# A two-layer graph network: finishing a block of attention by a narrow product, and the loads of the start over other queues

## The chip, the cores and the metric

The kernel runs on one core of a Trainium2 chip. A core has five engines that run their own instruction streams side by side: TensorE (PE: matmuls, and the loads of their stationary operand, PEld), VectorE (DVE), ScalarE (ACT), GpSimd (POOL) and SyncE (SP), which issues most of the DMAs. They share an on-chip memory (SBUF) and a smaller one into which TensorE writes (PSUM[...]). The metric is the device time of one execution in microseconds (us); smaller is better.

## The reference, cut

```python
# x: 3327 x 128, adj: 3327 x 3327 of zeros and ones; all float32
h = maximum(layernorm(x), 0)
deg = adj.sum(axis=1);  deg = where(deg == 0, 1, deg)
g = (adj.T @ h / deg) @ W_n.T + b_n + h @ W_c.T + b_c
x = x + relu(gamma * (g - mean(g)) * rsqrt(var(g) + 1e-5) + beta)   # over the nodes

h = maximum(layernorm(x), 0)
q, k, v = ((h @ W.T).reshape(128, 3327, 8) for W in (Wq, Wk, Wv))
a = einsum('dnh,dmh->dnm', q, k) * 128 ** -0.5 + adj + adj
out = einsum('dnm,dmh->dnh', softmax(a, axis=2), v)
x = x + out.reshape(3327, 1024) @ Wo.T
```

The second layer is an attention with 128 batches of 3327 queries by 3327 keys and only 8 numbers per query and key. Over a billion exponentials are taken, and nearly all of the time lies there.

## The kernel before

**The first layer** loads x, normalises it in 26 chunks of 128 nodes (stats, roots, factors, normalise, lines 342 to 367) and then runs over the 26 row chunks of adj (line 426): each is loaded by SP into one of three buffers, multiplied by TensorE into seven banks, summed by ScalarE and searched for its maximum by VectorE. `beside` adds small work of other kinds to each chunk. The loop over line 380 asks for the statistics of chunk group i + 1 before it normalises group i. All loads of x and of the weights are issued by ScalarE (lines 320 to 334), ahead of its first activation. Then come the batch norm, the residual, the second layer norm and the first projections (lines 461 to 612); `keep_nodes` stores x to the tensor xd, `keep_columns` the normalised x to hd, and the last loop sorts the keys of the first batches into `k`.

**The attention** (line 667) handles four batches at a time: 32 groups i, each of 7 blocks y of 476 queries (the last has 472), each block of 13 steps s. A step handles two chunks of keys, as four pairs of a key chunk and a half (two batches). For each pair TensorE makes the scores in two products of 32 rows (`product`, line 742), in one of three score buffers. Two or three of the four pairs are "plain": VectorE adds a chunk of adj (`add`, line 852), and one ScalarE row, `late`, takes the exponentials of all of them at line 895, one step later. The other one or two are "weighted": ScalarE takes the exponential straight from PSUM (line 861) and GpSimd multiplies by a stored exp(2 adj) (line 864, tile wt, loaded from the tensor wd). Steps 3, 7 and 11 (DOUBLE) have two weighted pairs, the others one. Three steps later (LAG) TensorE multiplies the exponentials by the values into one of two banks av (`weigh`, line 618), with a ninth value column of ones that gives the sum.

The order of the instructions is written out by hand; every engine works its own stream in that order. Within one step it is: the first weighted product and its exponential, `late` of the step before, product and add 0, the first half of the weighting (`second(0)`), product and add 1, the last product, then one `step()` of a finished block if s is in PARTS, the second half of the weighting, and a `begin` or `go_on` of a side job.

A finished block goes through the generator `finish` (line 623), one part per step of PARTS: copy av to SBUF (`avs`, step 3), four transposes that bring every fourth query onto the partitions (line 633, step 5), reciprocal and product with it (lines 640 to 643, result oq, step 7), store (step 8). Transposed, each of 119 partitions holds 128 columns per quarter, of which 4 x 9 mean something.

Side jobs are started in steps 7 and 11 of a block and use the bank av of the block that is being finished: six projections (queries, keys and values) for group i + 2 in blocks 0 to 2, two transposing parts of `outputs` for the group before in block 3, and its last part, the product with Wo in 16 matmul rows (line 277), in step 7 of block 4. In group 0 `more_weights` (line 755) also prepares the wd of the next block: it loads adj into a tile t in one step, takes its exponential on ScalarE in the next (line 770) and stores it in the one after.

SP works its queue in order too: `fetch` loads adj and wt two steps ahead and waits there for a free buffer, and each store waits for what it stores.

Of the kernel before, what the change touches and what calls it, by code (L numbers as in the profile page):

```python
# [9 lines left out]
F32 = mybir.dt.float32  # L10
# [9 lines left out]
D = 128  # L20
H = 8
# [12 lines left out]
CH = 4 * NP // D  # L34
NG = D // G
DOUBLE = (3, 7, 11)
PARTS = (3, 5, 7, 8)

# [8 lines left out]
def tile_two_layer_gnn(  # L47
# [206 lines left out]
    def outputs(wk, j):  # L254

        r = min(CH, N - j * CH)
        t = wk.tile([P, H, D], F32, name="t4")
        nc.sync.dma_start(
            t[:CH].rearrange("p e j -> p (e j)"), atr[j * CH : (j + 1) * CH, :]
        )  # L260
        xj = wk.tile([P, D], F32, name="xj")
        nc.sync.dma_start(xj[:CH], xd[j * CH : (j + 1) * CH, :])
        tT = wk.tile([P, H, P], F32, name="t4")

        def turn(e):
            bank = yield
            pt = bank.rearrange("p (i q) -> p i q", i=4)
            for i in range(4):
                nc.tensor.transpose(pt[:, i, :CH], t[:CH, 4 * e + i, :], ident[:CH, :CH])
            yield  # L270
            nc.vector.tensor_copy(tT[:, 4 * e : 4 * e + 4, :CH], pt[:, :, :CH])
            yield

        def last():
            bank = yield
            for e in range(H):
                nc.tensor.matmul(  # L277
                    bank[:CH, :D], tT[:, e, :CH], wo[:, e, :], start=(e == 0), stop=(e == H - 1)
                )
            yield  # L280
            y = wk.tile([P, D], F32, name="y")
            nc.vector.tensor_add(y[:CH], bank[:CH, :D], xj[:CH])
            yield
            for p0, p1 in pieces(r):
                nc.sync.dma_start(out[j * CH + p0 : j * CH + p1, :], y[p0:p1])

        return [turn(0), turn(1), last()]

    def drive(part, bank=None):

# [7 lines left out]
    with tc.tile_pool(name="l0", bufs=1) as l0, tc.tile_pool(  # L298
# [20 lines left out]

        xr = x[: (NC - 1) * P, :].rearrange("(c p) d -> p c d", p=P)  # L320
        nc.vector.memset(xs[:, NC - 1, :], 0.0)
        for c0, c1 in ((0, 8), (8, NC - 1)):
            nc.scalar.dma_start(xs[:, c0:c1, :], xr[:, c0:c1, :])
        for p0, p1 in pieces(N - (NC - 1) * P):
            nc.scalar.dma_start(
                xs[p0:p1, NC - 1, :], x[(NC - 1) * P + p0 : (NC - 1) * P + p1, :]
            )
        nc.scalar.dma_start(wc, WcT)
        for i, b in enumerate((b_n, b_c, gamma, beta)):
            nc.scalar.dma_start(cols[:, i : i + 1], b.rearrange("o d -> d o"))  # L330
        nc.scalar.dma_start(wn, WnT)
        for t, w in zip(wqk, (WqT, WkT, WvT)):
            nc.scalar.dma_start(t, w)
        nc.scalar.dma_start(wo, WoT.rearrange("(e p) o -> p e o", p=P))

        st = l0.tile([P, NC, 6], F32, name="ln_st")
        mv = l0.tile([P, NC, 2], F32, name="ln_mv")
# [45 lines left out]
        nc.vector.tensor_add(bias, cols[:, 0:1], cols[:, 1:2])  # L383

        def beside(x):

            if x < NQ:
                pt, cs = turned(x, A, aside)
                nc.scalar.copy(B[:, cs, :], pt)
            elif x < 2 * NQ:  # L390
                n0 = (x - NQ) * NB
                w = min(NB, NP - n0)
                nc.tensor.matmul(
                    aside[:, :w], wc, B2[:, n0 : n0 + w], start=True, stop=True
                )
                nc.scalar.activation(
                    C2[:, n0 : n0 + w], aside[:, :w], AF.Identity, bias=bias
                )
            elif x < 2 * NQ + 4:
                i = x - 2 * NQ  # L400
                sq = sp.tile([P, NB], F32, name="sq")
                w = wqk[i // 2][:, i % 2 * NB : (i % 2 + 1) * NB]
                nc.gpsimd.tensor_tensor(sq, w, w, ALU.mult)
                nc.tensor.matmul(aside[:1, :], ones[:, :1], sq, start=True, stop=True)
                nc.vector.tensor_reduce(norm[:, i : i + 1], aside[:1, :], AX.X, ALU.max)
# [128 lines left out]
        def residual(i):  # L534
            pt, cs = turned(i, A, acc[i])
            nc.vector.tensor_add(xs[:, cs, :], xs[:, cs, :], pt)
            if i < 2:
                keep_nodes(cs)

        def second_norm(i, engine):  # L540
# [82 lines left out]
    def finish(rp, av, d0, n0, w):  # L623
# [4 lines left out]
        nc.vector.tensor_copy(avs[:, : R * J], av[:, : R * J])  # L628
        yield

        pt = av.rearrange("p (j q) -> p j q", j=J)
        for j in range(J):
            nc.tensor.transpose(  # L633
                pt[:R, j, :], avs[:, j : j + (R - 1) * J + 1 : J], ident
            )
# [31 lines left out]
    def attention():  # L667


        with tc.tile_pool(name="adj", bufs=4) as ap, tc.tile_pool(  # L670
# [13 lines left out]
            if True:  # L684
# [69 lines left out]

                def more_weights(i, y, s):

                    k, phase = s // 3, s % 3
                    if i or y + 1 >= len(qblocks) or k > 3:
                        return
                    n0, w = qblocks[y + 1]  # L760
                    c = WC + 2 * k
                    n = min(2, NC - c)
                    if phase == 0:
                        have["w"] = wk.tile([P, 2, QB], F32, name="t4")
                        nc.sync.dma_start(
                            have["w"][:, :n, :w], adjr[:, c : c + n, n0 : n0 + w]
                        )
                    elif phase == 1:
                        a = have["w"][:, :n, :w]
                        nc.scalar.activation(a, a, AF.Exp, bias=low, scale=2.0)  # L770
                    else:
                        nc.sync.dma_start(
                            wd[c - WC : c - WC + n, :, n0 : n0 + w].rearrange("c p n -> p c n"),
                            have["w"][:, :n, :w],
                        )

# [53 lines left out]
                for x, (i, y, s) in enumerate(steps):  # L830
# [152 lines left out]
    def general():  # L983
# [65 lines left out]
        with tc.tile_pool(name="gw2", bufs=2) as wk, tc.tile_pool(  # L1049
            name="gp2", bufs=1, space=PSUM  # L1050
        ) as gp:
            banks = [gp.tile([P, NB], F32, name=f"h{i}") for i in range(3)]
# [52 lines left out]
```

## Time and profile before

| | us |
|---|---|
| median of 3 runs | 10390.24 |
| their range | 10385.12 to 10391.82 |
| the profiled execution | 10385.98 |
| its span, first to last instruction | 10384.2 |

| engine | busy us | share of the span |
|---|---|---|
| ScalarE | 9925.5 | 96% |
| TensorE | 9816.7 | 95% |
| VectorE | 9331.0 | 90% |
| GpSimd | 8443.5 | 81% |

A row of the list of groups gives a source line, engine, operation and tiles (written <- read), the shape, how many (x), then busy us and mean ns of one, then the idle time of the engine just before these instructions and what ended it. A row of the list of waits reads: who waited, for whom, us in total, how often, the longest. A row of the timeline reads: start and duration in us, engine, line, operation, tiles, shapes, how many rows are merged in it, and in brackets the engine's idle time before and what ended it. TensorE's durations are modelled and overlap; the distance between starts says more. The TensorE clock was granted at 0.991 of full speed on average.

### The profile page before, as it was taken

The numbers are of one execution on the slowest core, as the hardware profiler recorded it, in microseconds if no ns is written. First come the engines' busy times: TensorE is split into PE (matmuls) and PEld (weight loads), VectorE is DVE, ScalarE is ACT, GpSimd is POOL, SyncE is SP. The second block draws the span as 40 slices with busy tenths as digits, with TensorE's granted clock in tenths as the row PEclk, the third lists the DMA queues.
The fourth block names the chain that finished last, engine by engine and source line by source line (L and its number), as shares of the span: only waits on it lengthen the run. The fifth ranks groups of instructions, "written<-read, shape, count | busy, mean of one in ns | idle before, by whom it ended". The sixth has DMA issues, their size and how long they took to land.

```text
span 10384.2 us, 188013 instructions
## 1 busy us (share of the span) xinstructions
PE 9816.7 (95%) x72431; PEld 2888.6 (28%) x72431; DVE 9331.0 (90%) x9501; ACT 9925.5 (96%) x6655; POOL 8443.5 (81%) x4316
## 2 busy tenths in 40 slices
PE   7899999999999999999999999999999999999998
PEld 3222222222222222222222222222222222222222
DVE  5689999999999999999999999999999999999998
ACT  4789999999999999999999999999999999999998
POOL 1678888888888888888888888888888888888887
PEclk9899999999999999999999999999999999999999
DMA  6765666665666665666655666655666555666554
GB/s 232 205 178 161 164 168 167 168 165 158 168 167 168 167 162 161 168 169 168 167 159 163 168 169 167 164 165 159 171 168 167 162 164 164 169 168 165 159 153 129
DMA packets 1115994, 1735.87 MB, mean 167 GB/s; under 512 B 194606, under 2 KB 1091756, under 8 KB 1107404
## 3 DMA queue, kind: packets, MB, share of 16 engines
q1 hardware_dynamic: 1110558, 1717.86, 60.2%
q8 instruction: 568, 9.31, 0.4%
q10 hardware_dynamic: 4350, 4.20, 0.1%
q14 instruction: 342, 2.80, 0.1%
q0 software_dynamic: 176, 1.71, 0.0%
HBM read 1621.05 MB, written 102.38 MB: 166 GB/s over the span
## 4 chain that ended last, share of the span: by engine, by line
POOL 21%; PE 16%; ACT 8%; issue 5%; DVE 3%; DMA 0%; POOLq 0%; ACTq 0%; SPq 0%; DVEq 0%
POOL f L864 20%; PE av L618 8%; PE s L742 6%; ACT f L861 5%; ACT d L895 3%; DVE d L852 2%; PE av L633 1%; POOL k L192 1%; PE av L208 1%; PE av L277 0%; POOL o L238 0%; POOL o L237 0%; DVE oq L643 0%; DVE ri L641 0%; DVE avs L628 0%
## 5 line engine op out<-in xcount | busy, mean ns | idle before, releaser
L864 POOL TENSOR_TENSOR f<-f,wt 128x952 f32<-128x952 f32 (+1 forms) x3584 | 7944.8, 2235 | 1680.6 <-ACT f L861 1660.7
L852 DVE SCALAR_TENSOR_TENSOR d<-at,s 128x952 f32<-128x952 f32 x8064 | 8754.4, 1140 | 606.2 <-PE s L742 447.7
L895 ACT ACTIVATE d<-d 128x2856 f32<-128x2856 f32 (+1 forms) x2912 | 7055.5, 2423 | 12.5 <-DVE d L852 2.3
L618 PE MATMUL av<-d,v 128*9 128x476 f32 x32256 | 5072.3, 567 | 1.9 <-ACT d L895 1.9
L742 PE MATMUL s<-q,k 32*128 32x476 f32 x23296 | 4108.3, 476 | 407.9 <-ACT f L861 334.1
L861 ACT ACTIVATE f<-s 128x952 f32<-128x952 f32 (+1 forms) x3584 | 3436.4, 980 | 224.7 <-PE s L742 220.9
L742 PEld LDWEIGHTS s<-q,k 32*128 32x128 f32 x23296 | 1772.8, 182 | 5631.8 <-DVE d L852 3296.9
L618 PE MATMUL av<-f,v 128*9 128x476 f32 x14336 | 2853.4, 566 | 0.0
L618 PEld LDWEIGHTS av<-d,v 128*9 128x9 f32 x32256 | 583.6, 88 | 1162.3 <-issue 1131.8
L618 PEld LDWEIGHTS av<-f,v 128*9 128x9 f32 x14336 | 316.6, 88 | 153.1 <-issue 139.6
L192 POOL CAST k<-ks 128x256 fp32r<-128x256 f32 x434 | 284.6, 656 | 0.0
L633 PE MATMUL av<-ident,avs 128*119 128x128 f32 (+1 forms) x896 | 241.3, 392 | 0.8 <-DVE avs L628 0.8
L633 PEld LDWEIGHTS av<-ident,avs 128*119 128x119 f32 (+1 forms) x896 | 198.2, 292 | 52.7 <-issue 51.1
L430 PE MATMUL acc<-a,A 128*128 128x512 f32 (+1 forms) x364 | 151.8, 570 | 23.2 <-ACT A L364 23.1
L238 POOL TENSOR_TENSOR o<-pf,o 104x512 fp32r<-104x512 f32 x124 | 159.9, 1289 | 9.9
L628 DVE COPY avs<-av 128x476 f32<-128x476 f32 (+1 forms) x224 | 144.6, 645 | 4.5 <-PE av L618 4.5
L437 DVE TENSOR_REDUCE amax<-a 128x1 f32<-128x3327 f32 x26 | 93.7, 3611 | 35.3 <-DMA a<-in_adj 35.3
L236 DVE TENSOR_SCALAR pf<-av,low_half 104x512 f32<-104x512 f32 x62 | 46.6, 751 | 72.0 <-PE av L208 70.3
L234 DVE COPY pf<-av 104x512 f32<-104x512 f32 x62 | 42.9, 692 | 73.0 <-PE av L208 71.8
L214 DVE COPY ov<-av 104x512 f32<-104x512 f32 x62 | 42.9, 692 | 67.8 <-PE av L208 67.8
L430 PEld LDWEIGHTS acc<-a,A 128*128 128x128 f32 x364 | 69.0, 192 | 108.3 <-issue 84.7
L770 ACT ACTIVATE t<-t,low_half 128x952 f32<-128x952 f32 (+1 forms) x24 | 26.2, 1090 | 65.4 <-DMA t<-in_adjT 65.4
(121 smaller groups left out, 1022.6 us busy)
## 6 DMA issues: line engine op xcount, KB each, us to landing
at<-in_adjT SPq DMA_DIRECT2D x1728, 476.0 KB
wt<-wd SPq DMA_DIRECT2D x1536, 238.0 KB
at<-in_adjT SPq DMA_DIRECT2D x288, 472.0 KB
wt<-wd SPq DMA_DIRECT2D x256, 236.0 KB
ks<-kT SPq DMA_DIRECT2D x496, 104.0 KB
q<-qT SPq DMA_DIRECT2D x496, 104.0 KB
a<-in_adj SPq DMA_DIRECT2D x26, 1663.5 KB
kT<-o SPq DMA_DIRECT2D x128, 208.0 KB
```

The source lines that it names most:

```text
L192: nc.gpsimd.tensor_copy(k[:, c : c + n, half * 64 : half * 64 + 64], ks.bitcast(F32).rearrange("g (p c) -> g c p", c=NC)[:, c : c + n, :],)
L208: nc.tensor.matmul(bank[:CH], hj, wqk[s][:, e * NB : (e + 1) * NB], start=True, stop=True)
L238: nc.gpsimd.tensor_tensor(o[:CH, 1], f[:CH], o[:CH, 0].bitcast(F32), ALU.subtract)
L430: nc.tensor.matmul(acc[i][:, :w], A[:, c, :], a[:, n0 : n0 + w], start=(c == 0), stop=(c == NC - 1),)
L618: nc.tensor.matmul(av[32 * b : 32 * b + H + 1, :w], tiles[2][:, b, c, :], e, start=first, stop=last,)
L628: nc.vector.tensor_copy(avs[:, : R * J], av[:, : R * J])
L633: nc.tensor.transpose(pt[:R, j, :], avs[:, j : j + (R - 1) * J + 1 : J], ident)
L742: nc.tensor.matmul(p[:, x, :we], k[rs, c, :], q[rs, n0 : n0 + we], start=True, stop=True,)
L852: nc.vector.scalar_tensor_tensor(d[:, j, :, :w], have[0, i, y, c // 2][:, c % 2, :w] .unsqueeze(1).to_broadcast([P, 2, w]), SAFE / 2, p[:, ...
L861: nc.scalar.activation(f[:, :, :w], p[:, :, :w], AF.Exp, scale=2.0)
L864: nc.gpsimd.tensor_tensor(f[:, :, :w], f[:, :, :w], have[1, i, y, c][:, :w].unsqueeze(1).to_broadcast([P, 2, w]), ALU.mult,)
L895: nc.scalar.activation(flat, flat, AF.Exp, scale=2.0)
```

## The change

It has many small parts.

- `finish` replaces the four transposes by four ordinary matmuls against `some`, the 36 of the 128 columns of the identity that are used later, and makes them in two parts of two. PARTS gets a fifth step, 6, for the second.
- In step 7, the second of DOUBLE, `step()` stands before the second product and add instead of behind the last product.
- The last part of `outputs` becomes two, of four matmuls (eight rows) each, with an add of their own.
- `more_weights` takes the exponential in the third step of its three instead of the second, and stores a tile when it loads the next.
- The first four chunks of x are loaded by SP ahead of adj, the rest by ScalarE in other pieces; the weights are loaded by GpSimd; ScalarE's table of roots is loaded by an activation on a constant, ahead of the first that needs it; the sum of the biases moves into `beside`.
- Chunks 8 to 11 of xd are stored with those before them, the rest by GpSimd right after the residual; hd is stored after the sorting of the keys. The loads of the rest of q begin two steps later.

```diff
-PARTS = (3, 5, 7, 8)
+PARTS = (3, 5, 6, 7, 8)
...
-        def last():
+        def last(i):
             bank = yield
-            for e in range(H):
+            for e in range(4 * i, 4 * i + 4):
                 nc.tensor.matmul(
-                    bank[:CH, :D], tT[:, e, :CH], wo[:, e, :], start=(e == 0), stop=(e == H - 1)
+                    bank[:CH, :D], tT[:, e, :CH], wo[:, e, :],
+                    start=(e == 4 * i), stop=(e == 4 * i + 3),
                 )
             yield
-            nc.vector.tensor_add(y[:CH], bank[:CH, :D], xj[:CH])
+            nc.vector.tensor_add(y[:CH], bank[:CH, :D], y[:CH] if i else xj[:CH])
...
-        return [turn(0), turn(1), last()]
+        return [turn(0), turn(1), last(0), last(1)]
...
-        for c0, c1 in ((0, 8), (8, NC - 1)):
+        nc.sync.dma_start(xs[:, :4, :], xr[:, :4, :])
+        for c0, c1 in ((4, 12), (12, NC - 1)):
             nc.scalar.dma_start(xs[:, c0:c1, :], xr[:, c0:c1, :])
...
-        nc.scalar.dma_start(wc, WcT)
+        root = l0.tile([P, 1], F32, name="root")
+        nc.scalar.activation(root, eps, AF.Sqrt)
+        for t, w in zip(wqk, (WqT, WkT, WvT)):
+            nc.gpsimd.dma_start(t, w)
+        nc.gpsimd.dma_start(wc, WcT)
         for i, b in enumerate((b_n, b_c, gamma, beta)):
-            nc.scalar.dma_start(cols[:, i : i + 1], b.rearrange("o d -> d o"))
-        nc.scalar.dma_start(wn, WnT)
-        for t, w in zip(wqk, (WqT, WkT, WvT)):
-            nc.scalar.dma_start(t, w)
-        nc.scalar.dma_start(wo, WoT.rearrange("(e p) o -> p e o", p=P))
+            nc.gpsimd.dma_start(cols[:, i : i + 1], b.rearrange("o d -> d o"))
+        nc.gpsimd.dma_start(wn, WnT)
+        nc.gpsimd.dma_start(wo, WoT.rearrange("(e p) o -> p e o", p=P))
...
-            if i < 2:
+            if i < 3:
                 keep_nodes(cs)
...
+        nc.gpsimd.dma_start(
+            xd.rearrange("(c p) d -> p c d", p=P)[:, 12:, :], xs[:, 12:, :]
+        )
         roots(4, NC)
...
-        keep_nodes(slice(8, NC))
-        keep_columns(0, NQ)
         for x, c in enumerate(range(0, NC, 4)):
...
+        keep_columns(0, NQ)
...
-        pt = av.rearrange("p (j q) -> p j q", j=J)
+        pt = av[:, : J * G * (H + 1)].rearrange("p (j q) -> p j q", j=J)
+
+        some = ident.rearrange("p (b h) -> p b h", h=32)[:, :, : H + 1]
         for j in range(J):
-            nc.tensor.transpose(
-                pt[:R, j, :], avs[:, j : j + (R - 1) * J + 1 : J], ident
-            )
-        yield
-        pv = pt.rearrange("p j (b h) -> p b j h", h=32)
+            nc.tensor.matmul(
+                pt[:R, j, :], avs[:, j : j + (R - 1) * J + 1 : J], some, start=True, stop=True
+            )
+            if j % 2:
+                yield
+        pv = pt.rearrange("p j (b h) -> p b j h", h=H + 1)
...
-                    k, phase = s // 3, s % 3
-                    if i or y + 1 >= len(qblocks) or k > 3:
+                    k, phase = divmod(s, 3)
+                    if i or y + 1 >= len(qblocks):
                         return
                     n0, w = qblocks[y + 1]
                     c = WC + 2 * k
-                    n = min(2, NC - c)
+                    if phase == 0 and k:
+                        nc.sync.dma_start(
+                            wd[c - 2 - WC : c - WC, :, n0 : n0 + w].rearrange("c p n -> p c n"),
+                            have["w"][:, :, :w],
+                        )
+                    if c == NC:
+                        return
...
-                    elif phase == 1:
+                    elif phase == 2:
...
-                    for args in others[:2]:
-                        nc.sync.dma_start(*args)
-                    del others[:2]
+                    if x > 1:
+                        for args in others[:2]:
+                            nc.sync.dma_start(*args)
+                        del others[:2]
...
                     second(0)
+                    if s == DOUBLE[1]:
+                        step()
                     add(1, product(i, y, *plain[1]))
...
-                    if s in PARTS:
+                    if s in PARTS and s != DOUBLE[1]:
                         step()
...
-                for p, b in zip(outputs(wk, NG - 1), (0, 1, 0)):
+                for p, b in zip(outputs(wk, NG - 1), (0, 1, 0, 1)):
```

More of the change, by code (lines that the diff above doesn't have):

```diff
@@ L272, in turn @@
             yield
-        def last():
+        y = wk.tile([P, D], F32, name="y")
+        def last(i):
             bank = yield
-            for e in range(H):
+            for e in range(4 * i, 4 * i + 4):
                 nc.tensor.matmul(
-                    bank[:CH, :D], tT[:, e, :CH], wo[:, e, :], start=(e == 0), stop=(e == H - 1)
+                    bank[:CH, :D], tT[:, e, :CH], wo[:, e, :],
+                    start=(e == 4 * i), stop=(e == 4 * i + 3),
                 )
             yield
-            y = wk.tile([P, D], F32, name="y")
-            nc.vector.tensor_add(y[:CH], bank[:CH, :D], xj[:CH])
+            nc.vector.tensor_add(y[:CH], bank[:CH, :D], y[:CH] if i else xj[:CH])
             yield
-            for p0, p1 in pieces(r):
-                nc.sync.dma_start(out[j * CH + p0 : j * CH + p1, :], y[p0:p1])
-        return [turn(0), turn(1), last()]
+            if i:
+                for p0, p1 in pieces(r):
+                    nc.sync.dma_start(out[j * CH + p0 : j * CH + p1, :], y[p0:p1])
+        return [turn(0), turn(1), last(0), last(1)]
     def drive(part, bank=None):
@@ L382, in tile_two_layer_gnn @@
             normalise(i, A)
-        nc.vector.tensor_add(bias, cols[:, 0:1], cols[:, 1:2])
         def beside(x):
@@ L390, in beside @@
             elif x < 2 * NQ:
+                if x == NQ:
+                    nc.vector.tensor_add(bias, cols[:, 0:1], cols[:, 1:2])
                 n0 = (x - NQ) * NB
@@ L765, in more_weights @@
                         nc.sync.dma_start(
-                            have["w"][:, :n, :w], adjr[:, c : c + n, n0 : n0 + w]
+                            have["w"][:, :, :w], adjr[:, c : c + 2, n0 : n0 + w]
                         )
-                    elif phase == 1:
-                        a = have["w"][:, :n, :w]
+                    elif phase == 2:
+                        a = have["w"][:, :, :w]
                         nc.scalar.activation(a, a, AF.Exp, bias=low, scale=2.0)
[L771 to L774, printed above, removed]
-                        )
                 extra, begun = [], []
@@ L1051, in general @@
         ) as gp:
-            banks = [gp.tile([P, NB], F32, name=f"h{i}") for i in range(3)]
+            banks = [gp.tile([P, NB], F32, name=f"h{i}") for i in range(4)]
             for j in range(NG):
```

## The prediction

> **What bounds the kernel now.** I read the page first, then the list of waits, then the timeline, from which I took the start of every ScalarE row of the attention loop (lines 861 and 895) and so the length of every step.
>
> ```profile
> PE 9816.7 (95%) x72431; PEld 2888.6 (28%) x72431; DVE 9331.0 (90%) x9501; ACT 9925.5 (96%) x6655; POOL 8443.5 (81%) x4316
> L895 ACT ACTIVATE d<-d 128x2856 f32<-128x2856 f32 (+1 forms) x2912 | 7055.5, 2423 | 12.5 <-DVE d L852 2.3
> L861 ACT ACTIVATE f<-s 128x952 f32<-128x952 f32 (+1 forms) x3584 | 3436.4, 980 | 224.7 <-PE s L742 220.9
> ```
>
> Two engines look full, but only one is. The two ScalarE lines run back to back (a 0.96 us f row is followed after 0.84 us) and are busy 96%; d hardly ever waits (12.5 us of idle), f waits 224.7 us, and nearly all of that for a product of TensorE. TensorE's 95% is modelled overlap: a plain step issues its 8 products and 16 weighting passes in about 2.65 us (5018.92 to 5021.57 in the timeline) of the 3.32 us that a step lasts. So ScalarE's exponentials set the pace, and TensorE matters where it is late. The waits:
>
> ```profile
> ACT f L861 <- PE s L742: 220.9, 343, 3.8
> PEld av L208 <- DVE oq L643: 134.0, 92, 1.5
> ACT t L770 <- DMA t<-in_adjT: 65.4, 13, 10.1
> ```
>
> Where are the 220.9 us? I averaged step lengths over groups 3 to 29. Undisturbed plain steps last 3.32 us, a double one 4.16 and the step after it 2.53. The excess sits in few places: step 5, in blocks 0 to 6, by 0.49, 0.82, 0.83, 0.83, 0.84, 0.86 and 0.91 us (5.58 per group); step 7 in blocks 0, 1, 2 by 0.47 each and in block 4 by 1.35; step 9 by about 0.2 in blocks 0 to 4. The timeline shows what is late. Step 5 of a block of group 15, the four transposes of finish():
>
> ```profile
> 5021.57 1.14 PE L633 MATMUL av<-ident,avs 128*119 128x128 f32 x4
> ...
> 5024.12 0.96 ACT L861 ACTIVATE f<-s 128x944 f32<-128x944 f32 x1 [0.70 <-PE s L742]
> ```
>
> They hold TensorE 1.07 us from start to next row; f then idles 0.70. In block 0 the finished block is the narrow one, with 118 columns:
>
> ```profile
> 5065.73 0.71 PE L633 MATMUL av<-ident,avs 128*118 128x128 f32 x4
> ...
> 5067.86 0.96 ACT L861 ACTIVATE f<-s 128x952 f32<-128x952 f32 x1 [0.25 <-PE s L742]
> ```
>
> Here the hold is 0.64 and the idle 0.25. Both say: idle is the hold less about 0.4 us of slack. A stalled row also loses the 0.13 us overlap with its predecessor, so a step grows by hold - 0.4 + 0.13. Step 7, where a projection borrows the finished block's bank:
>
> ```profile
> 5073.87 0.29 DVE L643 TENSOR_TENSOR oq<-av,ri 118x128 f32<-118x128 f32 x1
> ...
> 5074.22 1.10 PE L208 MATMUL av<-wk,hj 128*104 128x512 f32 x2 [0.61 <-DVE oq L643]
> ...
> 5075.84 0.96 ACT L861 ACTIVATE f<-s 128x952 f32<-128x952 f32 x1 [0.36 <-PE s L742]
> ```
>
> TensorE waits 0.61 us for oq, projects for 1.04, and f is 0.36 late. In block 4 it is the last product of outputs() that follows the same wait, 16 rows in 1.93 us:
>
> ```profile
> 5253.21 2.00 PE L277 MATMUL av<-wo,t 128*104 128x128 f32 x16 [0.61 <-DVE oq L643]
> ```
>
> Two places come once. Group 0 lasts 412.6 us, the others 312.6; 65.4 of its excess is ScalarE at line 770, waiting for a load issued one step earlier:
>
> ```profile
> 395.29 1.09 ACT L770 ACTIVATE t<-t,low_half 128x952 f32<-128x952 f32 x1 [5.65 <-DMA t<-in_adjT]
> ```
>
> And the head, where TensorE is then busy without a break to 190 us:
>
> ```profile
> 13.61 0.87 DVE L345 BATCH_NORM_STATS2 ln_st<-xs 128x6 f32<-128x128 f32 x4 [12.18 <-DMA xs<-in_x]
> ...
> 20.56 1.28 ACT L352 ACT_TABLE_LOAD   x1 [19.16 <-issue]
> ...
> 23.14 13.63 PE L430 MATMUL acc<-a,A 128*128 128x512 f32 x28 [23.14 <-ACT A L364]
> ```
>
> [...] The trace agrees for an ordinary float32 load of 128: at line 485, where the matmul behind has 2 columns, the second load starts 0.108 us after the first. [...] Here such a product is two rows, each loading its weights[...], while a transpose is one row. [...] from 4 to 6 us SP's queue moved 56 rows of 13 KB and ScalarE's 57 packets of 512 B. [...] here hd was issued at 248.70 and its first packet ran at 254.09, so I use 5.4.
>
> **The change, part by part** (negative is time saved)
>
> Transposes as plain matmuls against 36 columns of the identity, two per step in steps 5 and 6. Four rows per half, each with a load of about 0.10 us; 36 columns[...] are 0.03 and hide behind the next load. Exposed first load 0.085 (the first interval of line 277 is 0.194 against 0.109 later), 4 x 0.10, a last 0.03, the change back 0.09: a hold of 0.60. Each of the 14 halves of a group then costs 0.60 - 0.40 + 0.13 = 0.33, say 0.34: 4.8 us against 5.58. Saved 0.8 per group, 26 in 32 groups. Unknown is the load: columns lie 16 bytes apart and 119 is odd, and in transpose mode that pair costs 0.218 a row where 118 costs 0.109. I take no penalty, because the weighting matmuls have 9 (odd) columns and load in 88 ns, 8 more than the 1-column load of line 404[...]. The bounds are a hold under 0.3 (all 178 us of stall gone, 152 more than I count) and 4 x 0.218 + 0.21 = 1.08.
>
> The normalisation (lines 640 to 643) moves ahead of the second add in step 7, some 1.1 us earlier. TensorE's 0.61 us wait for oq goes, which exceeds the 0.36 lateness: 0.47 in blocks 0, 1, 2, in 30 groups (the last two project nothing), 42 us. The add behind it ends 0.8 us later, near 5074.3, but d of that step starts only at 5076.70, so it hides; the projection's copy on VectorE, today idle 1.27 us for TensorE, comes earlier. Step 9's 0.2 is VectorE's lateness from that copy; I count 0.6 per group, 18 us.
>
> outputs() in two halves: 8 rows x 0.109 + 0.19 = 1.06 us in step 7, and again in step 11, where a projection of nearly that size (1.04) lengthens nothing (4.17). Block 4's 1.35 goes in 31 groups: 42 us. The extra add on VectorE (0.29) is covered by a wait of 2.09 for the product today.
> These last two parts: -102.
>
> Line 770 a step later (phase 2), the store at the next load. Without the first, the waits are 5.6, 5.7, 3.8, 6.0, 7.9 in step 1 and 4.0, 5.8, 0.9, 5.5, 6.3, 2.6 in step 10; less one step of 3.3 us they leave about 21 of 54. Saved 33; SP's queue may pass some on, so -30, between -10 and -55.
>
> Head. The first normalisation needs the second four chunks, still on ScalarE's queue; with turns taken packet by packet, and with the weights now beside them on GpSimd's, they land at 14 to 18 us. Then 1.2 on VectorE and some 2 through ScalarE, whose ten issues (5.9 us from 14.42) are gone and whose table is in. TensorE starts near 19 instead of 23.14: -4, between -7 and +1.
>
> Start of attention. xd leaves SP's queue, where the next issue sat 8.36 us behind it. But hd now follows GpSimd's sorting, which ended at 256.5; with 5.4 to its first packet and 4.6 of moving it lands at 266.5, and VectorE's first add waits for it, because d lies where B was. Today that add starts at 262.79, and the first d at 271.13 only because line 770 stood before it till 270.3. Then: 266.5 + 3.4 for three adds, 270. Nothing, between -6 and +5. Holding back the q loads for two steps is in this. The tail: nothing.
>
> Sum: -26 - 102 - 30 - 4 = -162. The profiled execution took 10385.98 us (span 10384.2), 4.3 below the median of 10390.24: 10224 against it, 10228 against the median.
>
> **Rivals.** (1) Slower: the load doubles for 119 columns outside transpose mode too. Hold 1.08, growth 0.83 as measured now, but in two steps: 12 x 0.83 + 2 x 0.34 - 5.58 = +5.1 per group, +162 instead of -26: 10416. Against it stand the 9-column loads; for it, that nothing here shows a strided ordinary load. The whole change turns slower from a hold of about 0.97. (2) The halves fit into the slack wholly: 10076. For it: a hold of 0.4 would do; against it, 0.64 leaves 0.25 idle. (3) Step 7 gains nothing, because the later add holds a score buffer or VectorE (90% busy) becomes the bound: 10228 + 102 = 10330. Against it: blocks with projections, less their stalls, last the same 43.3 us as blocks without.
>
> **How the numbers follow.** Forecast 0.58, with its own range 10170 to 10290; (1) 0.14, (2) 0.12, (3) 0.12, no net effect 0.04. No change means within 0.2%, 21 us. Faster 0.58 + 0.12 + 0.12 = 0.82, less 0.01 for edges; slower 0.14; same 0.05. The range takes in (2) and (3) and leaves (1) out: 10070 to 10340.
>
> **What would show it.** Line 208's and 277's waits for oq gone; idle before f in steps 6 and 7 of about 0.2 instead of 0.7 in 6; rows of the new transposes 0.10 apart; line 770's wait near 20 to 30; group 0 near 380, later groups near 308.5. Rows 0.2 apart and groups above 314 would prove me wrong, and so would a wait of d for VectorE.

## The result, and the profile after

| | median us | range | runs |
|---|---|---|---|
| before | 10384.39 | 10378.94 to 10391.82 | 20 |
| changed | 10379.0 | 10374.02 to 10385.02 | 20 |

The ratio is 0.9993, with a 95% interval from 0.9987 to 0.9999: a gain of 0.07%, where 1.6% was forecast; the prediction called anything within 0.2% no change. The profiled span went from 10384.2 to 10381.3 us. Read by stage (a group begins with its first f, the last stage runs to the end of the program), those 2.9 us are a balance of larger amounts:

| stage | before | changed | difference |
|---|---|---|---|
| start to the first f | 258.2 | 265.4 | +7.2 |
| group 0 | 412.6 | 390.8 | -21.8 |
| groups 1 to 30 | 9377.5 | 9385.1 | +7.6 |
| group 31 to the end | 335.9 | 340.0 | +4.1 |

Group 0 shrank, to 390.8 us where some 380 were foreseen. The steady groups should have gone to 308.5 us each, and stayed at 312.8. Engines and costliest rows of the page of the changed kernel:

```profile
PE 10000.7 (96%) x73327; PEld 3082.6 (30%) x73327; DVE 9367.7 (90%) x9533; ACT 9917.5 (96%) x6655; POOL 8442.6 (81%) x4327
...
L875 ACT ACTIVATE f<-s 128x952 f32<-128x952 f32 (+1 forms) x3584 | 3389.9, 968 | 283.4 <-PE s L754 268.2
...
L644 PE MATMUL av<-ident,avs 128*119 128x36 f32 (+1 forms) x1792 | 474.1, 391 | 0.8 <-DVE avs L637 0.8
```

ScalarE's wait for scores did not fall, it rose from 220.9 to 268.2 us, and line 644 is the suspect: 1792 rows, twice as many as the 896 transposes before. The waits of the changed kernel (total us, number, longest):

```profile
ACT f L875 <- PE s L754: 268.2, 426, 8.9
PEld av L208 <- DVE oq L655: 72.6, 91, 0.8
DVE d L866 <- DMA hd<-B: 15.6, 1, 15.6
ACT t L788 <- DMA t<-in_adjT: 13.5, 6, 4.9
```

The load's wait for oq was to go; it is 72.6 instead of 134.0, but what is left costs little, for step 7 now lasts 4.18 us against 4.16 for an undisturbed double step. The exponential (line 770 before, 788 now) waits 13.5 instead of 65.4. But there are 426 waits of f instead of 343: there is a new one. The timeline of steps 5 and 6 of one block (start, length, and in brackets the idle time before) names it:

```profile
5009.51 1.06 PE L644 MATMUL av<-ident,avs 128*119 128x36 f32 x4
...
5011.99 0.96 ACT L875 ACTIVATE f<-s 128x944 f32<-128x944 f32 x1 [0.62 <-PE s L754]
...
5013.41 1.06 PE L644 MATMUL av<-ident,avs 128*119 128x36 f32 x4
...
5015.90 0.96 ACT L875 ACTIVATE f<-s 128x944 f32<-128x944 f32 x1 [0.50 <-PE s L754]
```

The two halves stall ScalarE by 0.62 and 0.50 us, where the whole pass of four transposes had cost 0.70. The four rows of a half come 0.218 us apart, so it holds TensorE for 0.99 us, not 0.60. Averaged over groups 3 to 29 and all blocks but the last, step 5 lasts 4.06 to 4.10 us, step 6 3.92, and an undisturbed step 3.32; step 7 fell to 4.18, from 4.63 (blocks 0 to 2) and 5.51 (block 4).

### The profile page after: what moved, and what is told of

The parts are those of the page before. It is cut to its first block, busy times and chain, and to the rows that moved or that the text cites. A ratio compares the mean times of both kernels' runs of the same rounds, so it can differ in the third digit from the quotient of the medians.

```text
span 10381.3 us, 189923 instructions
## 1 busy us (share of the span) xinstructions
PE 10000.7 (96%) x73327; PEld 3082.6 (30%) x73327; DVE 9367.7 (90%) x9533; ACT 9917.5 (96%) x6655; POOL 8442.6 (81%) x4327
## 4 chain that ended last, share of the span: by engine, by line
PE 41%; POOL 23%; ACT 19%; issue 8%; DVE 1%; DMA 1%; SPq 0%; POOLq 0%; ACTq 0%; DVEq 0%
POOL f L878 22%; PE av L627 21%; PE s L754 14%; ACT f L875 12%; ACT d L911 7%; PE av L644 4%; PE av L208 1%; DVE d L866 1%; DMA at<-in_adjT 1%; POOL k L192 0%; POOL o L238 0%; DMA wt<-wd 0%; PE av L269 0%; DVE ov L214 0%; POOL o L237 0%
## 5 line engine op out<-in xcount | busy, mean ns | idle before, releaser
L875 ACT ACTIVATE f<-s 128x952 f32<-128x952 f32 (+1 forms) x3584 | 3389.9, 968 | 283.4 <-PE s L754 268.2
L754 PEld LDWEIGHTS s<-q,k 32*128 32x128 f32 x23296 | 1740.3, 182 | 5496.6 <-DVE d L866 3013.3
L644 PE MATMUL av<-ident,avs 128*119 128x36 f32 (+1 forms) x1792 | 474.1, 391 | 0.8 <-DVE avs L637 0.8
L644 PEld LDWEIGHTS av<-ident,avs 128*119 128x119 f32 (+1 forms) x1792 | 422.9, 308 | 103.2 <-issue 101.6
L441 ACT ACTIVATE junk<-a 128x3327 bf16<-128x3327 f32 x26 | 77.4, 2977 | 6.6 <-DMA a<-in_adj 6.5
```

Source lines behind the costliest of these rows:

```text
L644: nc.tensor.matmul(pt[:R, j, :], avs[:, j : j + (R - 1) * J + 1 : J], some, start=True, stop=True)
L754: nc.tensor.matmul(p[:, x, :we], k[rs, c, :], q[rs, n0 : n0 + we], start=True, stop=True,)
L875: nc.scalar.activation(f[:, :, :w], p[:, :, :w], AF.Exp, scale=2.0)
```

## The experiments

Each time is a median of 4 runs (20 where said), each ratio is against the kernel before on the same chip. The experiments ran on several chips, on which the kernel before takes 10384.4 to 10390.2 us, so a difference of two times is good to a few us where it crosses chips.

### 1. The transposes as before, all else changed

```
-PARTS = (3, 5, 6, 7, 8)
+PARTS = (3, 5, 7, 8)
...
-            nc.tensor.matmul(pt[:R, j, :], avs[:, j : j + (R - 1) * J + 1 : J], some, ...)
-            if j % 2:
-                yield
+            nc.tensor.transpose(pt[:R, j, :], avs[:, j : j + (R - 1) * J + 1 : J], ident)
+        yield
```

> The changed kernel with its transposes as before: four 128-column transposes in one part at step 5, no part at step 6; all else as changed. Theory (the two halves hold TensorE 0.99 and 0.98 us instead of the 0.60 I assumed, and that eats what step 7 gave back): steps 5 and 6 lose the 9.4 us a group that they are longer than plain steps now (1.35 us x 7 blocks) and take back 5.6 (0.79 x 7): -3.9 us in each of 32 groups, -124 us, near 10255. The row step 5 is 4.1 us again, step 6 3.32, step 7 stays near 4.2. Rival (the blocks are at ScalarE's own limit, busy 96% of the span, so time taken from TensorE can't come through): less than 30 us gained, 10350 to 10380, with the idle time before ScalarE's f moving to other steps.

Measured: 10250.85 us, ratio 0.9869 (0.9852 to 0.9885). Groups last 308.9 us, step 6 is 3.34, step 7 4.16. The wait of f for scores, and ScalarE's rows in steps 5 to 7 of one block:

```profile
ACT f L872 <- PE s L751: 167.4, 233, 8.9
```

```profile
5032.54 0.96 ACT L872 ACTIVATE f<-s 128x952 f32<-128x952 f32 x1 [0.67 <-PE s L751]
5033.40 2.58 ACT L908 ACTIVATE d<-d 128x2856 f32<-128x2856 f32 x1
5035.88 0.95 ACT L872 ACTIVATE f<-s 128x952 f32<-128x952 f32 x1
```

In the block shown one stall is left, 0.67 us after the pass, and the next f follows d at once. The theory stands: all the rest of the change saves 137.6 us (10388.4 - 10250.85), and the narrow halves cost about 130 against the pass that they replaced: 128 from the medians (10379.0 - 10250.85), 132 if each is first set against the kernel before on its own chip.

### 2. What makes the rows slow: stride, odd count or moving operand

The copy into avs writes each quarter's columns side by side. This edit alone went into the changed kernel, into the kernel of experiment 1, and into the kernel before.

```
-        nc.vector.tensor_copy(avs[:, : R * J], av[:, : R * J])
+        av4 = avs[:, : R * J].rearrange("p (j r) -> p j r", j=J)
+        nc.vector.tensor_copy(av4, av[:, : R * J].rearrange("p (r j) -> p j r", j=J))
...
-                avs[:, j : j + (R - 1) * J + 1 : J]
+                av4[:, j, :]
```

> The changed kernel, with only the order of the columns in avs altered: VectorE's copy writes each quarter's 119 columns side by side, so that each TensorE load reads them without the 16-byte stride. Theory stride (the load of 119 columns 16 bytes apart takes double): rows of these matmuls come 0.11 us apart instead of 0.218, the load row falls from 308 to about 200 ns, a half holds 0.60 us, steps 5 and 6 are 0.4 and 0.3 us shorter each: 0.7 x 7 x 32 = 155 us, near 10225; VectorE's copy at 0.65 us may grow by its strided reading, up to 1.2 us, which would give some 0 to 60 us back. Rival odd count (119 columns) or rival moving operand (36 columns in 4 runs of 9): the rows stay 0.218 apart and the time stays within 10 us of 10379, or rises with the copy.

> Both edits: transposes as before (transpose mode, 128 moving columns, one part at step 5) and the columns of avs side by side. Theory stride: the transposes' rows come 0.11 us apart instead of 0.218, the pass holds 0.64 us instead of 1.07, step 5 is 0.4 us shorter than in the run with the transposes back alone: 0.4 x 7 x 32 = 90 us, near 10165. Rival odd count (in the kernel before, 118 columns with the same stride came 0.11 apart in transpose mode and 119 came 0.218): side by side or not, 119 columns stay 0.218 apart, the pass holds 1.07 us, and the time is that of the run with the transposes back alone, near 10255.

> The kernel before, with only the order of the columns in avs altered, so that each transpose loads its 119 columns side by side. Theory (in transpose mode 119 columns 16 bytes apart take double, side by side they don't, whatever stands around them): rows 0.109 apart, the pass holds 0.63 us instead of 1.07, step 5 shrinks from 4.15 to 3.7: 0.42 x 6 x 32 = 80 us, near 10305. Rival (in the kernel before the time taken from step 5 comes back as a longer wait of step 7 for oq, in blocks 0, 1, 2 and 4): 0.42 x 2 x 32 = 27 us or so, near 10360.

| kernel, dense columns | us | ratio (interval) | forecast |
|---|---|---|---|
| changed | 10179.9 | 0.9799 (0.9783 to 0.9816) | 10225 |
| changed, transposes back | 10166.6 | 0.9787 (0.9770 to 0.9803) | 10165 |
| before | 10301.9 | 0.9920 (0.9903 to 0.9936) | 10305 |

Load rows with each shape kept apart (busy us, mean ns). Before, transposes, columns 16 bytes apart:

```profile
L633 PEld LDWEIGHTS av<-ident,avs 128*119 128x119 f32 x768 | 181.5, 309 | 44.0 <-issue 44.0
L633 PEld LDWEIGHTS av<-ident,avs 128*118 128x118 f32 x128 | 16.7, 195 | 8.7 <-issue 7.1 <-DVE avs L628 1.6
```

Changed, plain matmuls, the same columns:

```profile
L644 PEld LDWEIGHTS av<-ident,avs 128*119 128x119 f32 x1536 | 363.0, 309 | 87.4 <-issue 87.4
L644 PEld LDWEIGHTS av<-ident,avs 128*118 128x118 f32 x256 | 59.9, 307 | 15.8 <-issue 14.2 <-DVE avs L637 1.6
```

Changed with dense columns, plain matmuls:

```profile
L645 PEld LDWEIGHTS av<-ident,avs 128*119 128x119 f32 x1536 | 189.2, 183 | 87.0 <-issue 87.0
L645 PEld LDWEIGHTS av<-ident,avs 128*118 128x118 f32 x256 | 31.1, 181 | 15.8 <-issue 14.2 <-DVE avs L638 1.6
```

Dense columns with the transposes back:

```profile
L643 PEld LDWEIGHTS av<-ident,avs 128*119 128x119 f32 x768 | 97.4, 183 | 43.9 <-issue 43.9
L643 PEld LDWEIGHTS av<-ident,avs 128*118 128x118 f32 x128 | 13.1, 136 | 8.7 <-issue 7.1 <-DVE avs L638 1.6
```

Read the second form of each pair. A plain load of 118 columns takes 307 ns strided, as long as 119: the odd count is not the cause there. With dense columns (side by side) it is 181: the stride is. The moving operand is the same in both. In transpose mode 118 columns take less than 119 in either layout (195 against 309, 136 against 183). Within a part, rows behind the second come apart, in us, by:

| | 119 columns | 118 columns |
|---|---|---|
| plain, 16 bytes apart | 0.218 | 0.216 |
| plain, dense | 0.104 | 0.103 |
| transpose, 16 bytes apart | 0.218 | 0.111 |
| transpose, dense | 0.109 | 0.109 |

For plain loads the stride alone takes a row from 0.104 to 0.218 us (119 columns) and from 0.103 to 0.216 (118). Only these two layouts were run, so why a stride of 16 bytes costs this much, and what another would cost, was not shown.

The transposes of 118 columns, 0.111 against 0.109, look like an exception, but the starts of the loads in the same traces say otherwise. In transpose mode the second load of a part starts 0.196 us after the first with 119 strided columns and 0.101 with dense ones; with 118 it is 0.089 and 0.055. So the stride costs there too. It doesn't show in the rows of 118, because in these traces the rows of transposes with 128 moving columns come no closer than 0.109 us (with 104 moving columns, line 269, 0.089), and a load of 0.089 fits in between. Why 118 columns load in about half the time of 119 in transpose mode, and not as plain weights (0.194 and 0.196 strided), no run explains. The transposes of line 269 point to the even count: their 128 columns take 0.058. But 119 is the only odd count measured.

The copy lost nothing by its strided reading: for 476 columns 643 ns in the changed kernel with dense columns, 650 without (the 1.2 us that I had allowed for was a guess). The hold of a half fell to 0.535 us, and the waits of f for scores from 268.2 us to 55.6:

```profile
ACT f L876 <- PE s L755: 55.6, 159, 8.9
```

Step 5 then lasts 3.61 us and step 6 3.46: both shrank by 0.46, where I had set 0.4 and 0.3, so the first forecast came out 45 us too long. Even so, the narrow halves are 13 us slower than the one pass of transposes with the same dense columns (10179.9 against 10166.6). The load of about 0.10 us that the prediction assumed fits the dense rows (0.104) and not the strided ones (0.218).

### 3. What the rest gave: order, outputs, exponential

From the kernel of experiment 1, first the normalisation after the last add again:

```
-                    if s == DOUBLE[1]:
-                        step()
...
-                    if s in PARTS and s != DOUBLE[1]:
+                    if s in PARTS:
```

> The kernel with the transposes back, and in addition the normalisation of step 7 after the step's last add again, as before. Theory (the wait of TensorE for oq is what the order removed, 0.45 us in step 7 of blocks 0, 1, 2 and 0.2 in step 9, as these steps stood before): 0.65 x 3 to 4 blocks x 31 groups = 60 to 80 us lost, near 10320, step 7 of blocks 0 to 2 at 4.6 us instead of 4.16. Rival (the gain of step 7 came from cutting the outputs in two): within 10 us of 10251.

Then, instead, the outputs in one piece and the exponential a step earlier:

```
-        return [turn(0), turn(1), last(0), last(1)]
+        return [turn(0), turn(1), last()]
...
-                    elif phase == 2:
+                    elif phase == 1:
```

> The kernel with the transposes back, and in addition the outputs in one piece and the weights' exponential one step after its load, as before. The two meet in different places, so they are read apart: the outputs in block 4 of groups 1 to 31, the exponential in group 0. Theory: step 7 of block 4 grows from 4.16 to 5.5, 1.34 x 31 = 42 us; the waits of the exponential for its load rise from 14 to some 55 to 65 us and group 0 from 380 to about 410, 30 us; total near 10323. Rival for group 0 (its gain is that of the projections, not of the exponential): group 0 within 5 us of 380 and the total near 10293. Rival for the outputs (half of the product still waits as long as the whole): block 4 less than 0.5 us longer.

The waits that came back, of the first and of the second run:

```profile
PEld av L208 <- DVE oq L652: 135.4, 92, 1.9
```

```profile
ACT t L776 <- DMA t<-in_adjT: 60.9, 14, 8.0
```

Order: 10332.3 us, ratio 0.9949 (0.9932 to 0.9965), so 81.5 over experiment 1. Step 7 is 4.63 again in blocks 0 to 2 and 4.64 in block 4, and step 9 3.5 in blocks 0 to 4. The other two: 10306.8, ratio 0.9924 (0.9908 to 0.9941), so 56.0 over it: block 4 lasts 45.11 instead of 44.24 (0.87 x 31 = 27), group 0 409.8 instead of 380.4 (29.4), with the exponential's wait. The three parts together make 137.5 of the 137.6 us, which is closer than the few us to which times from two chips compare. The outputs' share is two thirds of the forecast one, because in the kernel before 0.48 of block 4's 1.35 belonged to the order.

### 4. The start: loads, weights and hd

First the changed kernel with the loads as before (20 runs):

```
-        nc.sync.dma_start(xs[:, :4, :], xr[:, :4, :])
-        for c0, c1 in ((4, 12), (12, NC - 1)):
+        for c0, c1 in ((0, 8), (8, NC - 1)):
...
-            nc.gpsimd.dma_start(t, w)      # and the other weights
+            nc.scalar.dma_start(t, w)
```

> The changed kernel with the first loads as before: x in two large pieces and then the weights, all over ScalarE's queue, no activation on the constant, the sum of the biases before the loop. Theory (the head's loop lost its 4.9 us to these loads: its end is at 195.0 instead of 190.1): loop end near 190, first f near 260.5, total near 10374. Rival (the loads cost nothing and the loop's 4.9 us come from elsewhere): loop end near 195, first f near 265, total 10379 or, if the earlier x had helped, up to 4 us more.

Then the kernel of experiment 1 with the weights on nc.scalar but x in three pieces, and keep_columns before the sorting:

```
-            nc.gpsimd.dma_start(t, w)      # and the other weights
+            nc.scalar.dma_start(t, w)
...
+        keep_columns(0, NQ)
         for x, c in enumerate(range(0, NC, 4)):
...
-        keep_columns(0, NQ)
```

> The kernel with the transposes back, and in addition the weights over ScalarE's queue behind x again (x itself as changed), and hd written before the sorting again. The two are read apart: the head's loop in the time of its last row, hd in the first steps. Theory: without transfers of the weights on GpSimd's queue beside x the second piece of x lands earlier, the first maxima start near 31.7 us instead of 34, the loop ends at 190 instead of 192.6 and the first f starts near 260; without the late hd, VectorE's wait of 17.8 us for it goes, step 1 of the first block has 2 to 3 us of idle time instead of 9.3, and the total falls by 8 to 10, to 10242. Rival (hd's lateness is hidden by the sorting that delays the first f, as I had predicted): the idle time moves ahead of the first f, which then starts near 266, and the total stays at 10251 within 3 us.

And the best kernel (below) with x in two pieces as it has it, but the weights over GpSimd's queue and the activation on the constant:

```
+        nc.scalar.activation(root, eps, AF.Sqrt)
-            nc.scalar.dma_start(t, w)      # and the other weights
+            nc.gpsimd.dma_start(t, w)
```

> The kernel of the best run (halves at steps 4 and 6), with x in two pieces over ScalarE's queue as before, but the weights over GpSimd's queue and the activation on the constant, as changed. Theory (the weights on a queue of their own take turns with x's packets, and x lands later): the first row of VectorE's maxima starts at 33.7 to 35.1 us as in the seven runs with the changed loads, instead of 31.5 to 31.9 as in the five with the loads of before; the loop ends at 192 to 195 and the total is 2 to 5 above 10082. Rival (it is the cutting of x, with its first piece on SP's queue ahead of the adjacency): maxima at 31.9 or earlier, loop end at 190.3 or earlier, total 10077 to 10082.

| kernel | x | weights over | first maxima | loop ends | us |
|---|---|---|---|---|---|
| changed | three pieces | GpSimd | 34.7 | 195.0 | 10379.0 |
| loads back | two | ScalarE | 31.5 | 190.3 | 10376.5 |
| weights and hd back | three | ScalarE | 34.9 | 193.6 | 10246.9 |
| best, weights over GpSimd | two | GpSimd | 39.9 | 198.3 | 10092.8 |
| best | two | ScalarE | 31.9 | 190.3 | 10081.7 |

"First maxima" is the start of VectorE's first row of maxima, "loop ends" that of the first row behind the loop over adj. All five kernels with both loads of before end the loop at 190.1 to 190.3, all seven with both loads of the change at 192.3 to 195.3. So the head lost 2 to 5 us; in the total this can't be told from nothing (ratio with the loads back 0.9990, 0.9983 to 0.9997). The last pair differs in the weights' queue, and besides only in their order and in the activation on the constant, a row of 0.20 us: with the same x, moving the weights to GpSimd's queue costs 8 us in the loop and about 7 in all (the profiled spans are 10086.2 and 10079.4; of the 11 between the medians, 4 lie between the chips). The direction was forecast, the size more than twice as large. VectorE's first statistics of x in that kernel:

```profile
25.55 0.87 DVE L350 BATCH_NORM_STATS2 ln_st<-xs 128x6 f32<-128x128 f32 x4 [24.11 <-DMA xs<-in_x]
```

In the best kernel these rows start at 13.68: x lands 12 us later when the weights move beside it. The issue of its last small pieces holds ScalarE's queue (ACTq) for 24.1 us, in the best kernel for 12.2 (second row):

```profile
2.31 24.07 ACTq L328 DMA_DIRECT2D xs<-in_x  x2
...
2.31 12.18 ACTq L328 DMA_DIRECT2D xs<-in_x  x2
```

In the changed kernel three queues carry loads at once, and from 8 to 14 us they moved about as many packets each, as turns would give: SP's 154 (1.84 MB), GpSimd's 157 (0.55 MB), ScalarE's 159 (0.08 MB). VectorE takes the statistics of the first four chunks, over SP's queue, at 4.25 and of the next four at 6.94, but ScalarE can't go on with them. ScalarE's queue in the changed kernel, issues (ACTq) included:

```profile
1.97 18.38 ACTq L329 DMA_DIRECT2D xs<-in_x  x2
20.38 1.28 ACT L334 ACT_TABLE_LOAD   x1 [20.38 <-issue]
...
28.88 0.30 ACT L359 ACTIVATE ln_sd<-ln_mv,eps 128x4 f32<-128x4 f32 x1 [2.59 <-DVE ln_mv L354]
```

Issuing the last pieces of x holds ScalarE's queue for 18.4 us, so the table for the constant is loaded no earlier than the one for the roots was before (20.56). Later ScalarE waits 2.6 us for the statistics of chunks 12 and on, and VectorE for their piece of x. What makes an issue last so long no run shows.

The run with the weights back on ScalarE's queue disproved the first half of its theory: the loop was to end at 190 and ended at 193.6, because the issues of the weights then kept ScalarE from the first root until 25.15. The second half, on hd, held only in place. Step 1 of the first block idles 2.97 us instead of 9.31 and that block lasts 52.7 instead of 61.1, but later blocks of group 0 gave back 6.6. The total, ratio 0.9866 (0.9850 to 0.9883), is that of experiment 1 within its spread.

### 5. A better kernel

Dense columns, transposes in two parts of two; then with the loads of before and hd early; then at other steps:

```
-        yield
+            if j % 2:
+                yield
...
-PARTS = (3, 5, 7, 8)
+PARTS = (3, 5, 6, 7, 8)      # in the last run (3, 4, 6, 7, 8)
```

> The kernel with dense columns and the transposes back, and in addition the four transposes in two parts of two, at steps 5 and 6. Theory (a hold up to about 0.4 us fits into the slack of a step): a half holds 0.41 us instead of 0.63 for all four, its step grows by 0.0 to 0.14 instead of 0.38: (0.38 - 0.2) x 224 = 40 us, or up to 85 if nothing is left; 10082 to 10130, most likely 10125. Rival (a part costs a fixed time however small, because it stands before the next scores): no gain, 10150 to 10180.

> The kernel with the dense columns and two parts of two transposes, with the first loads as before and hd written before the sorting. Theory (both are separate from the blocks): the head's loop ends at 190 instead of 192.3, the wait of VectorE for hd of 18 us goes, first f and first group together are 5 to 9 us shorter than 646.4, blocks as they were at 304.6 a group; near 10112. Rival (group 0 gives it back in the waits of its later blocks, as it did with the transposes back): 644 to 647, near 10117.

> The kernel of the run before (loads as before, hd early, dense columns), with the two halves of the transposes at steps 4 and 6 instead of 5 and 6. Theory (what is left of step 5's growth, 0.17 us, comes from following the short step 4 or from two halves in a row, and a half at step 6 costs nothing): up to 0.17 x 224 = 38 us gained, near 10075. Rival (at step 4 the half delays the scores that step 5 begins with just as much, or by more because the copy into avs has only one step): 10110 to 10150.

| | us | ratio (interval) | group |
|---|---|---|---|
| halves at 5 and 6 | 10119.2 | 0.9743 (0.9727 to 0.9759) | 304.6 |
| and loads back, hd early | 10109.8 | 0.9736 (0.9720 to 0.9752) | 304.7 |
| halves at 4 and 6 | 10081.7 | 0.9708 (0.9692 to 0.9724) | 303.7 |

A half of the first of these runs, in the timeline:

```profile
5016.99 0.48 PE L643 MATMUL av<-ident,avs 128*119 128x128 f32 x2
```

A half of two transposes holds TensorE for 0.41 us, a half of the narrow products with the same dense columns 0.535, since each of those is two rows, with a load for each. The same split, at the same steps, takes 10119.2 us with transposes and 10179.9 with narrow products. So in these runs the narrow product gained nothing; the cut into halves and the dense columns did. Narrow halves at other steps were not run.

At step 5 a half still lengthens its step by 0.17 (3.49 us). At step 6 it costs nothing (3.34, as without a half), nor at step 4 (2.52 us), where the first product of step 5 is issued early, ahead of the second half of the weighting. Why step 5 pays and the other two don't was not tested apart. The second run is 9.4 us shorter than the first; its trace has 9.6 less up to the end of group 0 (636.8 against 646.4). In the last, the wait of f for scores:

```profile
ACT f L870 <- PE s L749: 28.5, 21, 3.4
```

All 21 waits lie in group 0. In groups 1 to 30 no gap between ScalarE's rows exceeds 0.07 us: the steady groups run at ScalarE's own pace. From its page:

```profile
PE 9781.0 (97%) x72431; PEld 2819.0 (28%) x72431; DVE 9303.7 (92%) x9533; ACT 9871.1 (98%) x6655; POOL 8433.9 (84%) x4317
```

ScalarE is busy 98% of the span. Of the 208 us in which it isn't, 139 lie ahead of the first f, 47 in group 0 and nearly all of the rest behind the last row. This is the fastest kernel of the study.

## Why the prediction was wrong

- **The transposes: wrong, and it decided.** I counted -26 us, the runs say about +130. The step that failed is "I take no penalty" for columns 16 bytes apart: rows of 0.10 and a hold of 0.60 were 0.218 and 0.99. The formula of growth held in step 5 (0.99 - 0.40 + 0.13 = 0.72, measured 0.75) and gave 0.12 too much in step 6 (measured 0.60). With dense columns, where the rows are 0.104 apart as assumed, the same halves beat the strided pass by 71 us (10179.9 against 10250.85), more than the 26 counted. I had the fact before me, and read it wrongly. In transpose mode 118 strided columns were fast, so I took the stride for free and asked only whether an odd count hurts. But that load did pay (0.089 us against 0.055), and the pass of 128 columns, 0.111 a row, hid it; the narrow products are plain loads, 0.194 for the same 118 columns, with 36 moving columns to hide behind (about 0.03 us, an estimate from the 0.429 us that a row of 512 columns takes at line 430 of the kernel before). The 9-column loads (88 ns) that I called as a witness have their columns side by side. The prediction itself said that nothing here shows a strided ordinary load.
- **The first rival came near the price, not the cause.** It set the hold at 1.08, the total at 10416, and blamed 119 columns; 118 pay the same. The turning point, a hold of about 0.97, was nearly right: 0.99 still gave a gain of 0.07%.
- **Step 7: right in sum.** -102 forecast; undone singly, the order is worth 81.5 and the outputs 27, together 108.5. I had counted 60 for the order and 42 for the outputs: block 4's part of the order (0.48 a group) stood with the outputs, and step 9 gave in five blocks, not in three.
- **The exponential: right.** -30 forecast, 29.4 in group 0.
- **Head: wrong sign, small.** -4 was forecast, with TensorE starting near 19; it started at 23.47, and the loop ended 4.9 later. The second four chunks of x came even earlier than thought (statistics at 6.94, not 14 to 18). I had overlooked that issuing the last of x keeps ScalarE from using them until 20.4, and that the later pieces would come later beside the weights: the roots of chunks 12 to 15 are taken at 28.88 instead of 25.87. (The ten issues that were taken away had lasted 6.1 us, not 5.9.)
- **Start of attention: right, but for what the head passed on.** I put hd at 266.5 and the first d at 270, no loss. VectorE's first add did wait for hd, until 273.19, and the first d came at 276.54 instead of 271.13. Of these 5.4 us the loop's late end explains 4.9: from there to the first d it is 81.5 us, and was 81.0. The row, in the timeline of the changed kernel:

```profile
273.19 10.82 DVE L866 SCALAR_TENSOR_TENSOR d<-at,s 128x952 f32<-128x952 f32 x10 [15.58 <-DMA hd<-B]
```

- **Tail: small miss.** Nothing forecast, +4.1 in the last stage, which pays for the halves and projects nothing that could win it back; with the transposes back it takes 334.9 us, 1.0 less than before.

All but the transposes was to bring -136, and brought -137.6. That the two are so close is in part luck: the order's surplus made up for the outputs and for the head.

## What to carry to other kernels

In these runs an operand's stride was part of a TensorE load's price (rows 0.218 us apart against 0.104): let the copy that fills the tile lay the columns side by side, which cost VectorE nothing here (643 ns against 650). Moving fewer columns did not make a product cheaper where its loads set the pace: a transpose of 128 moving columns was one row, a plain product of 36 was two, and a dense half held TensorE for 0.41 us with transposes, for 0.535 with plain products. When one shape of an instruction is fast, ask which of its properties makes it so before carrying one of them over to another mode. Work put between TensorE's products was free only up to a slack of about 0.4 us (by estimate, from idle times of 0.70 after a hold of 1.07 and 0.25 after 0.64), so it was worth cutting to that size and placing where there is slack: a half of 0.41 us cost 0.17 at step 5 and nothing at steps 4 and 6.

## What the runs showed of the hardware

- Float32 weights whose columns lie 16 bytes apart took 1.6 to 2.1 times as long as dense ones. Plain: rows 0.218 against 0.104 us apart (119 columns), 0.216 against 0.103 (118). In transpose mode, second load after the first: 0.196 against 0.101 (119), 0.089 against 0.055 (118).
- In transpose mode 118 columns loaded in about half the time of 119 (0.055 against 0.101 us, dense), 128 columns in 0.058; plain loads of 118 and 119 columns differed by 0.002 or less.
- Dense transposes came 0.109 us apart with 128 moving columns, 0.089 with 104; with 118 columns and 128 moving, loads of 0.055 us (dense) and of 0.089 (strided) left the rows 0.109 and 0.111 apart.
- A plain float32 product of the finished block was two rows, each with its load, a transpose one (1792 against 896 rows); rows of 512 moving columns came 0.429 us apart (line 430 of the kernel before).
- VectorE's copy out of PSUM with a 16-byte stride took 643 ns for 476 elements, against 650 without.
- ScalarE was held 18.4 us by the issue of two small last pieces of x (56 and 7.5 KB); with the rest of x in two pieces instead of three it was 24.1 us beside weights on GpSimd's queue, and 12.2 with the weights behind x on its own.
- DMA queues with loads at the same time moved about as many packets each, whatever their size: in the changed kernel 154, 157 and 159 from 8 to 14 us, at 1.84, 0.55 and 0.08 MB.
